# Four image layers on one core: another order of the seven block products and their banks, more background slots in layer 2, first k and v by seven products, order of the last divisions

## Chip, cores and metric

The kernel runs on one core of one Trainium2 chip. The metric is the device time of one execution in microseconds, the median of three runs. TensorE's granted clock was 0.995 of full speed in the profiled run.

## What is computed

The input x has 4 images of 512 channels and 1024 positions, all in four byte floats. Four layers change it in turn, and each adds its result to x:

- Layer 0: attention with 8 heads of 64 channels, with biases; then an output projection.
- Layer 1: linear attention with 64 softplus features. `KV = Kf V^T`, `wval = Qf KV / (Qf sum(Kf))`, V scaled by a gate of maximum plus mean of x; x becomes `x + gamma * wval`.
- Layer 2: layer norm over channels, attention with one head of 512, projection.
- Layer 3: group norm (32 groups), attention with 4 heads of 128, projection.

```python
qkv = xs @ Wp.T + bp                       # layers 0, 2, 3: three 512x512 products an image
attn = softmax(q @ k.T * hd ** -0.5)
x = x + (attn @ v) @ Wo.T + bo
```

A projection of one image is a product of a 512x512 weight with a 512x1024 activation.

## The kernel before, in words

**Tiles.** x of all four images stays on the chip. A *block* is 128 x 4 x 512: one weight, or half an image (512 positions) of q, k, v or of a normalised x; there are 12 block buffers. Exponentials lie in five `pt` tiles of 128 x 2 x 512. In PSUM there are two `acc` tiles of one bank, two `sc` tiles of two banks each, two `tr` tiles of one bank. A wait for an sc tile is for the whole tile of two banks.

**Projections by seven products.** `two_by_sevens` (L312) cuts the weight and the activation into 2 x 2 blocks and computes the four result blocks from seven block products, not eight (a form of Strassen's method). The list `SEVEN` (L264) says for each product: its number, its bank, whether the result is put (copied, by ScalarE) or added (by VectorE), and to which block. A bank is not cleared between some products, so that sums build up in it. Each call works on two column blocks (`which` 0 and 1), each with one acc tile as bank 0 and the two halves of an sc tile as banks 1 and 2. Each product is two matmuls for each `which`. `channels_first` (L333) makes q and k and, with its own put and add, the output projection `project_out` (L403); `tokens_first` (L352) makes v, with 256 columns a matmul. The sums of weight blocks come from `weight_sums` (L271; four VectorE operations), in layers 0 and 3 once a weight and kept in DRAM (`keep_sums`, L373); the sums of activation blocks come from `right` (L295; four VectorE operations of 128 x 1024, lines 303 to 306).

**The first image of layer 0** uses `first_qkv` (L217), with plain products: q and k of the first half are built in all eight banks at once, chunk by chunk as x, wq and wk arrive; then v of that half, then q, k and v of the second half, four matmuls a bank.

**Attention** (L442). A step is 128 keys of a head pair (layer 0), or 256 keys of a head. In `run`, two steps of scores are issued (L470), then the values (L503) of the two steps before; ScalarE makes the exponential (L477), VectorE adds the exponentials up (L481, L485). When a head is done, `normalize` (L549) is put off by two slots: `denominators` (L529) sums over partitions with a matmul, takes the reciprocal (L541), checks the denominators into `stat` (L542) and returns; then the values are multiplied (L552), which frees their acc tile. With one head (layer 2), `values_of_one` (L512) makes the four output blocks from four steps at once (L518) and divides them (L525). On the last half of the last image the output projection is plain: three of four chunks for each output block, `flush()` of what was put off, then the fourth chunk.

**Background work.** Layer norm, group norm, linear attention and the preparation of layer 3's weights are generators; `slot()` (L155) runs the first in the list by one step. Slots lie between products, between attention steps and in `values_of_one`. `finish()` runs what is left. A layer norm needs 13 steps for an image, a group norm 8, `prepare` (L897) 17. A scheduler then orders the instructions of each engine by their dependences and by its own estimate of times[...].

Of the kernel before, what the change touches and what calls it, by code (L numbers as in the profile page):

```python
# [17 lines left out]
P = 128  # L18
B = 4
C = 512  # L20
# [34 lines left out]
def conv_fast(ctx: ExitStack, tc: tile.TileContext, d: dict, out: bass.AP, flag):  # L55
# [47 lines left out]
    cols = const.tile([P, NCOLS], F32, name="cols")  # L103
    nc.sync.dma_start(cols, d["cols"])
    w0 = [block(n) for n in ("wq", "wk", "wv")]
    for c in range(NC):
        nc.sync.dma_start(xs[0][:, c, :TB], xin[0, :, c, :TB])
        for w, part in ((w0[0], 0), (w0[1], 1)):
            nc.sync.dma_start(w[:, c, :], by_chunk(d["wqkv0"])[:, c, part * C : (part + 1) * C])
    nc.sync.dma_start(w0[2], by_chunk(d["wqkv0"])[:, :, 2 * C : 3 * C])  # L110
    nc.sync.dma_start(xs[0][:, :, TB:], xin[0, :, :, TB:])
    wo = load("wo", d["wo0"])
    for b in range(1, B):
        nc.sync.dma_start(xs[b], xin[b])
# [99 lines left out]
        else:  # L214
            nc.vector.tensor_copy(dst, ps)

    def first_qkv(w, bias, xb):  # L217

        q, k, v = [], [], []
        for tb in range(NTB):
            x = xb[tb]
            q.append(block("q"))
            k.append(block("k"))
            v.append(block("v"))
            if tb == 0:

                banks = [s[:, i, :] for s in (sc_tile(), sc_tile()) for i in range(2)]
                banks += [acc_tile() for _ in range(2)] + [tr_tile() for _ in range(2)]
                for c in range(NC):
                    for o in range(2 * NC):
                        product(
                            banks[o], lambda c: w[o // NC][:, c, bass.ts(o % NC, P)],
                            lambda c: x[:, c, :], [c],
                        )
                for o in range(2 * NC):
                    evict(o, (q, k)[o // NC][tb][:, o % NC, :], banks[o], col(bias, o))  # L240
            else:
                for o in range(2 * NC):
                    ps = acc_tile()
                    product(
                        ps, lambda c: w[o // NC][:, c, bass.ts(o % NC, P)], lambda c: x[:, c, :]
                    )
                    slot()
                    evict(o, (q, k)[o // NC][tb][:, o % NC, :], ps, col(bias, o))
            for t in range(QT):
                ps = acc_tile()  # L250
                product(ps, lambda c: x[:, c, bass.ts(t, P)], lambda c: w[2][:, c, :])
                slot()
                evict(t, v[tb][:, t, :], ps)
        return q, k, v

# [4 lines left out]


    SEVEN = [  # L264
        (1, 0, "put", (0, 0)), (2, 1, "add", (0, 0)), (7, 2, "put", (1, 1)), (6, 0, "put", (1, 0)),
        (4, 2, "add", (1, 0)), (5, 0, "add", (1, 1)), (3, 0, "put", (0, 1)),
    ]
    HC = NC // 2
    HO = C // 2
# [42 lines left out]
    def two_by_sevens(factors, n, put, add):  # L312


        banks = []
        for _ in range(2):
            pair_of = sc_tile()
            banks.append([acc_tile()[:, :n], pair_of[:, 0, :n], pair_of[:, 1, :n]])
        for i, bank, do, block_of in SEVEN:
            for which in range(2):  # L320
                ps = banks[which][bank]
                for j in range(HC):
                    lhs, rhs = factors(which, i, j)

                    first = i in (1, 2, 7)
                    nc.tensor.matmul(  # L326
                        ps, lhsT=lhs, rhs=rhs, start=first and j == 0, stop=(j == HC - 1),
                        skip_group_check=not first,
                    )
                (put if do == "put" else add)(which, block_of, ps)  # L330
            slot()

    def channels_first(a, b, out, put=None, bias=None):  # L333
# [39 lines left out]
    def keep_sums(key, w):  # L373

        t = weight_sums(w, "wsum")
        kept = dram.tile([P, NC, TB], F32, tag=key, name="kept")
        nc.sync.dma_start(kept, t)
        sums_in_dram[key] = kept

    def load_left(key, src, part=0):  # L380
        w = load("w", src, part)
# [21 lines left out]
    def project_out(att, a):  # L403


        b = right(att.q, [lambda: pair("t3"), lambda: pair("t2"), pt_tile], over=True)

        def put(which, at, ps):
            o = 2 * at[0] + which
            att.add_to_x(at[1], o, ps, done=(at == (0, 1)))  # L410

        def add(which, at, ps):
            o = 2 * at[0] + which
            xv = xs[att.b][:, o, bass.ts(at[1], TB)]
            nc.vector.tensor_tensor(xv, ps, xv, ALU.add)
            att.store_x(at[1], o)

        def factors(which, i, j):
            return a[i][:, j, bass.ts(which, P)], b[i][:, j, :]

        two_by_sevens(factors, TB, put, add)

    def project_qkv(loads, bias, xb, before):

        x = right(xb, [pt_tile] * 4)
        q = [block("q") for _ in range(NTB)]
        channels_first(loads.take("q"), x, q, bias=lambda o: col(bias, o))
        if before is not None:
            loads.start("k")
            project_out(before, loads.take("o"))  # L430
            loads.start("v")
        else:
            loads.start("v")
        if before is not None and before.then is not None:
            background.append(before.then())
        k = [block("k") for _ in range(NTB)]
        channels_first(loads.take("k"), x, k, bias=lambda o: col(bias, NC + o))
        v = [block("v") for _ in range(NTB)]
        tokens_first(loads.take("v"), x, v)
        return q, k, v  # L440

    class Attention:  # L442
# [69 lines left out]
        def values_of_one(s, i):  # L512
            qb, g, j = s.steps[i]
            parts = [s.pts.pop(i - s.per + 1 + n) for n in range(s.per)]
            for n in range(NC):
                ps = acc_tile()
                for key in range(NT):
                    nc.tensor.matmul(  # L518
                        ps, lhsT=s.v[key // QT][:, key % QT, bass.ts(n, P)],
                        rhs=parts[key // 2][:, key % 2, :],  # L520
                        start=(key == 0), stop=(key == NT - 1),
                    )
                if n == 0:
                    r = s.denominators(qb, g)
                nc.vector.tensor_tensor(ps, ps, r, ALU.mult)  # L525
                s.add_to_x(qb, n, ps)
                slot()

        def denominators(s, qb, g):  # L529
            t = s.sums.pop((qb, g))  # L530
            ps = tr_tile("den")
            if s.pair:
                for half in range(2):
                    nc.tensor.matmul(  # L534
                        ps[half * s.hd : (half + 1) * s.hd, :], lhsT=ones[:, : s.hd],
                        rhs=t[:, half, :], start=True, stop=True,
                    )
            else:
                nc.tensor.matmul(ps, lhsT=ones, rhs=t[:, 0, :], start=True, stop=True)  # L539
            r = work.tile([P, TB], F32, tag="r", bufs=2, name="r")  # L540
            nc.vector.reciprocal(r, ps)  # L541
            nc.vector.scalar_tensor_tensor(  # L542
                ps, ps, 0.0, r, ALU.add, ALU.add,
                accum_out=stat[:, n_units[0] : n_units[0] + 1],
            )
            n_units[0] += 1
            return r

        def normalize(s, qb, g):  # L549

            r = s.denominators(qb, g)
            nc.vector.tensor_tensor(s.q[qb][:, g, :], s.accs.pop((qb, g)), r, ALU.mult)  # L552
            if s.last and g == s.groups - 1 and qb < NTB - 1:
                later(3, lambda: s.project_out(qb))

# [21 lines left out]
        def run(s):  # L577


            for i in range(0, len(s.steps) + 2, 2):  # L580
                for n in range(i, i + 2):
                    if n < len(s.steps):
                        s.scores(n)
                for n in range(i - 2, i):
                    if n >= 0:
                        s.values(n)
                if not s.one or i % s.per:
                    slot()
            if s.last:

# [1 line left out]
                banks = [t[:, i, :] for t in (sc_tile(), sc_tile()) for i in range(2)]  # L592
                for o in range(NC):
                    s.out_product(banks[o], s_last, o, range(NC - 1))
                flush()
                for o in range(NC):
                    s.out_product(banks[o], s_last, o, [NC - 1])
                    s.add_to_x(s_last, o, banks[o])
# [234 lines left out]
        norms[key] = []  # L833
        background.append(norm(b, norms[key]))

    def idle(n):
        for _ in range(n):
            yield


# [2 lines left out]
    for b in range(B):  # L843
        xb = [xs[b][:, :, bass.ts(tb, TB)] for tb in range(NTB)]
        if b == 0:
            for key, w in zip(("q0", "k0", "v0", "o0"), w0 + [wo]):
                keep_sums(key, w)
            q, k, v = first_qkv(w0, "bqkv0", xb)
            eb = column_sums(wo, "bqkv0", 2, "bo0")
            wv1 = load("wv1", d["wv1"])  # L850
            w1 = block("w1")
# [60 lines left out]
    for b in range(B):  # L912
# [7 lines left out]
            finish()  # L920
            start_norm(layer_norm, b + 1, f"ln{b + 1}")
        else:
            start_norm(group_norm, 0, "gn0")
            background.append(prepare())
        Attention(b, q, xn, v, 1, None, eb).run()
        finish()

# [501 lines left out]
```

## Time and profile before

The median is 2649.06 us (2648.99 to 2651.49); the profiled execution took 2642.78 us, its span on the core 2641.1 us.

| part of the profile | busy or total |
|---|---|
| VectorE, ScalarE | 1410.6 us (53%), 690.1 us (26%) |
| chain that ended last: TensorE, VectorE, ScalarE, issue | 92%, 4%, 2%, 1% |
| block products of all projections in the chain (L326) | 18% + 12% |
| reciprocals of denominators (L541), 72 of 3356 ns | 241.7 us |
| data moved | 100.44 MB, 38 GB/s in the mean |

PE is TensorE, DVE is VectorE, ACT is ScalarE, SP issues most transfers. In a row such as `acc<-ptt,ws` the tile before the arrow is written. A row of the table of waits reads: engine, tile and line that waited `<-` engine, tile and line that ended the wait. A row of the timeline gives start, length, engine, line, operation, tiles and shapes, and in brackets the idle time before it. A matmul leaves two records.

### The profile page before, as it was taken

The numbers are of one execution on the slowest core, as the hardware profiler recorded it, in microseconds if no ns is written. First come the engines' busy times: TensorE is split into PE (matmuls) and PEld (weight loads), VectorE is DVE, ScalarE is ACT, GpSimd is POOL, SyncE is SP. The second block draws the span as 40 slices with busy tenths as digits, with TensorE's granted clock in tenths as the row PEclk, the third lists the DMA queues.
The fourth block names the chain that finished last, engine by engine and source line by source line (L and its number), as shares of the span: only waits on it lengthen the run. The fifth ranks groups of instructions, "written<-read, shape, count | busy, mean of one in ns | idle before, by whom it ended". The sixth has DMA issues, their size and how long they took to land.

```text
span 2641.1 us, 19557 instructions
## 1 busy us (share of the span) xinstructions
PE 2584.7 (98%) x7818; PEld 1174.1 (44%) x7818; DVE 1410.6 (53%) x1637; ACT 690.1 (26%) x881; POOL 2.1 (0%) x12
## 2 busy tenths in 40 slices
PE   9999999999999999999999999989999999999998
PEld 4333533353335334544544545435445444544543
DVE  2486477646864887426345153252762563365254
ACT  0342244134412541212211112012321321231220
POOL 0000000000000000000000000000000000000000
PEclk9999999999999999999999999999999999999999
DMA  8001000100010001000000000041012002102000
GB/s 310 33 1 64 32 32 1 64 32 32 1 64 32 0 1 64 1 0 0 1 0 0 1 0 32 16 175 64 0 48 80 32 32 80 48 0 96 16 0 33
DMA packets 35953, 100.44 MB, mean 38 GB/s; under 512 B 2448, under 2 KB 2960, under 8 KB 31248
## 3 DMA queue, kind: packets, MB, share of 16 engines
q1 hardware_dynamic: 33552, 94.94, 10.0%
q10 hardware_dynamic: 2304, 4.20, 0.4%
q8 instruction: 63, 1.03, 0.2%
q14 instruction: 34, 0.28, 0.0%
HBM read 82.35 MB, written 16.78 MB: 38 GB/s over the span
## 4 chain that ended last, share of the span: by engine, by line
PE 92%; DVE 4%; ACT 2%; issue 1%; DMA 0%; SPq 0%; DVEq 0%; ACTq 0%
PE sc L470 25%; PE acc L326 18%; PE acc L503 17%; PE sc L326 12%; PE acc L518 8%; PE acc L202 3%; PE den L539 1%; PE sc L202 1%; PE z L628 1%; PE den L534 1%; PE wval L730 1%; PE kx L675 1%; DVE sum L485 1%; PE xtr L666 1%; PE po L202 1%
## 5 line engine op out<-in xcount | busy, mean ns | idle before, releaser
L477 ACT ACTIVATE ptt<-sc 128x1024 f32<-128x1024 f32 x416 | 411.9, 1022 | 748.3 <-PE sc L470 697.9
L470 PE MATMUL sc<-q,k 64*128 64x512 f32 (+1 forms) x1536 | 486.6, 610 | 7.2 <-ACT ptt L477 7.1
L503 PE MATMUL acc<-ptt,v 128*64 128x512 f32 (+1 forms) x1536 | 478.8, 603 | 0.0
L485 DVE TENSOR_TENSOR sum<-sum,ptt 128x1024 f32<-128x1024 f32 x272 | 331.1, 1217 | 231.3 <-ACT ptt L477 221.2
L470 PEld LDWEIGHTS sc<-q,k 64*128 64x128 f32 (+1 forms) x1536 | 184.5, 187 | 288.8 <-issue 197.9
L541 DVE RECIPROCAL r<-den 128x512 f32<-128x512 f32 x72 | 241.7, 3356 | 125.8 <-PE den L539 123.3
L503 PEld LDWEIGHTS acc<-ptt,v 128*64 128x64 f32 (+1 forms) x1536 | 160.0, 154 | 293.3 <-issue 290.7
L518 PE MATMUL acc<-ptt,v 128*128 128x512 f32 x512 | 223.7, 592 | 0.3 <-DVE x L567 0.3
L470 PE MATMUL sc<-q,ln 128*128 128x512 f32 x512 | 221.1, 592 | 0.0
L481 DVE TENSOR_TENSOR sum<-ptt 128x1024 f32<-128x1024 f32 x72 | 87.8, 1219 | 154.4 <-ACT ptt L477 154.2
L518 PEld LDWEIGHTS acc<-ptt,v 128*128 128x128 f32 x512 | 97.1, 190 | 122.6 <-issue 120.8
L470 PEld LDWEIGHTS sc<-q,ln 128*128 128x128 f32 x512 | 97.2, 190 | 120.3 <-issue 120.1
L367 DVE TENSOR_TENSOR v<-sc,v 128x256 f32<-128x256 f32 x88 | 37.3, 424 | 144.8 <-PE sc L326 143.1
L326 PE MATMUL acc<-ptt,ws 128*128 128x512 f32 x224 | 102.5, 595 | 0.0
L363 ACT COPY v<-acc 128x256 f32<-128x256 f32 x132 | 48.7, 372 | 148.1 <-PE acc L326 148.1
L344 ACT ACTIVATE k<-acc,cols 128x512 f32<-128x512 f32 x42 | 28.9, 687 | 215.2 <-PE acc L326 215.2
L567 DVE SCALAR_TENSOR_TENSOR x<-acc,cs,x 128x512 f32<-128x512 f32 x74 | 55.4, 749 | 51.9 <-PE acc L326 51.3
L326 PE MATMUL sc<-ptt,w 128*128 128x512 f32 x168 | 76.6, 594 | 0.0
L344 ACT ACTIVATE q<-acc,cols 128x512 f32<-128x512 f32 x42 | 28.9, 687 | 175.7 <-PE acc L326 175.7
L326 PEld LDWEIGHTS acc<-ptt,ws 128*128 128x128 f32 x224 | 42.1, 190 | 55.2 <-issue 50.7
L348 DVE TENSOR_TENSOR q<-sc,q 128x512 f32<-128x512 f32 x44 | 29.9, 679 | 68.1 <-PE sc L326 68.1
L348 DVE TENSOR_TENSOR k<-sc,k 128x512 f32<-128x512 f32 x28 | 19.4, 691 | 81.4 <-PE sc L326 81.4
(265 smaller groups left out, 2557.7 us busy)
## 6 DMA issues: line engine op xcount, KB each, us to landing
ws<-kept SPq DMA_DIRECT2D x28, 1024.0 KB, 4.8
w<-in_wqkv SPq DMA_DIRECT2D x24, 1024.0 KB, 5.0
kept<-wsum SPq DMA_DIRECT2D x8, 1024.0 KB, 10.1
w<-in_wo SPq DMA_DIRECT2D x7, 1024.0 KB, 5.3
x<-in_x SPq DMA_DIRECT2D x3, 2048.0 KB, 20.4
wo<-in_wo SPq DMA_DIRECT2D x4, 1024.0 KB, 6.3
out<-x SPq DMA_DIRECT2D x16, 256.0 KB, 2.0
out<-x ACTq DMA_DIRECT2D x16, 256.0 KB, 2.0
```

The source lines that it names most:

```text
L202: nc.tensor.matmul(ps, lhsT=lhs(c), rhs=rhs(c), start=(c == 0), stop=(c == NC - 1))
L326: nc.tensor.matmul(ps, lhsT=lhs, rhs=rhs, start=first and j == 0, stop=(j == HC - 1), skip_group_check=not first,)
L344: nc.scalar.activation(out[at[1]][:, o, :], ps, AF.Identity, bias=bias(o))
L348: nc.vector.tensor_tensor(c, ps, c, ALU.add)
L470: nc.tensor.matmul(ps[:, half, :], lhsT=s.k[key // QT][p0:p1, c, bass.ts(key % QT, P)], rhs=s.q[qb][p0:p1, c, :], start=(n == 0), stop=(n ...
L477: nc.scalar.activation(pt, ps, AF.Exp, scale=s.scale)
L481: nc.vector.tensor_tensor(t, s.pts[i - 1], pt, ALU.add)
L485: nc.vector.tensor_tensor(t, t, pt, ALU.add)
L503: nc.tensor.matmul(ps[p0:p1, :], lhsT=s.v[key // QT][:, key % QT, g * P + p0 : g * P + p1], rhs=pt[:, half, :], start=(key == 0), stop=(ke ...
L518: nc.tensor.matmul(ps, lhsT=s.v[key // QT][:, key % QT, bass.ts(n, P)], rhs=parts[key // 2][:, key % 2, :], start=(key == 0), stop=(key == ...
L541: nc.vector.reciprocal(r, ps)
L567: nc.vector.scalar_tensor_tensor(xv, ps, s.eb[:, o : o + 1], xv, ALU.add, ALU.add)
```

## The change

1. **Order and banks of the seven products.** The list begins with product 2. Product 3 gets a cleared bank 1 (it was added up in bank 0), product 5 comes last and its sum in bank 0 is added to two result blocks. So a call has four additions for each `which`, not three, and four copies as before. The aim is to have other products between the eviction of a tile and its next use. In `project_out` the store of the second half now follows the addition.
2. **First k and v by seven products.** `first_qkv` becomes `first_q`: q of both halves is built in the eight banks, chunk by chunk, and k and v come from `channels_first` and `tokens_first`. x of the first image is loaded in whole chunks.
3. **More slots in layer 2.** A slot after each score step and none after the values: 16 an image instead of 10. After the last image group norm and weight preparation advance side by side (`together`), one step of each in a slot.
4. **Last divisions.** The multiplication stands before the check everywhere (`check` is a function of its own), and at the very end the flush stands behind the first output block's three chunks.

```diff
-    SEVEN = [
-        (1, 0, "put", (0, 0)), (2, 1, "add", (0, 0)), (7, 2, "put", (1, 1)), (6, 0, "put", (1, 0)),
-        (4, 2, "add", (1, 0)), (5, 0, "add", (1, 1)), (3, 0, "put", (0, 1)),
-    ]
+    SEVEN = [
+        (2, 1, [("put", (0, 0))]), (1, 0, [("add", (0, 0))]), (7, 2, [("put", (1, 1))]),
+        (6, 0, [("put", (1, 0))]), (4, 2, [("add", (1, 0))]), (3, 1, [("put", (0, 1))]),
+        (5, 0, [("add", (1, 1)), ("add", (0, 1))]),
+    ]
...
-                    first = i in (1, 2, 7)
+                    more = i in (4, 5, 6)
...
-            att.add_to_x(at[1], o, ps, done=(at == (0, 1)))
+            att.add_to_x(at[1], o, ps, done=False)
...
     for c in range(NC):
-        nc.sync.dma_start(xs[0][:, c, :TB], xin[0, :, c, :TB])
-        for w, part in ((w0[0], 0), (w0[1], 1)):
-            nc.sync.dma_start(w[:, c, :], by_chunk(d["wqkv0"])[:, c, part * C : (part + 1) * C])
...
+        nc.sync.dma_start(xs[0][:, c, :], xin[0, :, c, :])
+        nc.sync.dma_start(w0[0][:, c, :], w0v[:, c, :C])
...
+    def first_q(w, bias, xb):
+        q = [block("q") for _ in range(NTB)]
+        banks = [s[:, i, :] for s in (sc_tile(), sc_tile()) for i in range(2)]
+        banks += [acc_tile() for _ in range(2)] + [tr_tile() for _ in range(2)]
+        for c in range(NC):
+            for n in range(2 * NC):
+                product(
+                    banks[n], lambda c: w[:, c, bass.ts(n // NTB, P)],
+                    lambda c: xb[n % NTB][:, c, :], [c],
+                )
...
-            q, k, v = first_qkv(w0, "bqkv0", xb)
+            q = first_q(w0[0], "bqkv0", xb)
+            x = right(xb, [pt_tile] * 4)
+            k = [block("k") for _ in range(NTB)]
+            channels_first(
+                left(w0[1], keep_sums("k0", w0[1])), x, k, bias=lambda o: col("bqkv0", NC + o)
+            )
+            v = [block("v") for _ in range(NTB)]
+            tokens_first(left(w0[2], keep_sums("v0", w0[2])), x, v)
+            keep_sums("q0", w0[0])
+            keep_sums("o0", wo)
...
                 if n == 0:
-                    r = s.denominators(qb, g)
+                    den, r = s.denominators(qb, g)
                 nc.vector.tensor_tensor(ps, ps, r, ALU.mult)
                 s.add_to_x(qb, n, ps)
+                if n == 0:
+                    s.check(den, r)
...
-            r = s.denominators(qb, g)
+            den, r = s.denominators(qb, g)
             nc.vector.tensor_tensor(s.q[qb][:, g, :], s.accs.pop((qb, g)), r, ALU.mult)
+            s.check(den, r)
...
                         s.scores(n)
+                        if s.one:
+                            slot()
...
-                if not s.one or i % s.per:
+                if not s.one:
                     slot()
...
                 for o in range(NC):
                     s.out_product(banks[o], s_last, o, range(NC - 1))
-                flush()
+                    flush()
...
-            start_norm(group_norm, 0, "gn0")
-            background.append(prepare())
+            norms["gn0"] = []
+            background.append(together(group_norm(0, norms["gn0"]), prepare()))
```

More of the change, by code (lines that the diff above doesn't have):

```diff
@@ L105, in conv_fast @@
     w0 = [block(n) for n in ("wq", "wk", "wv")]
+    w0v = by_chunk(d["wqkv0"])
     for c in range(NC):
-        nc.sync.dma_start(xs[0][:, c, :TB], xin[0, :, c, :TB])
-        for w, part in ((w0[0], 0), (w0[1], 1)):
-            nc.sync.dma_start(w[:, c, :], by_chunk(d["wqkv0"])[:, c, part * C : (part + 1) * C])
-    nc.sync.dma_start(w0[2], by_chunk(d["wqkv0"])[:, :, 2 * C : 3 * C])
-    nc.sync.dma_start(xs[0][:, :, TB:], xin[0, :, :, TB:])
+        nc.sync.dma_start(xs[0][:, c, :], xin[0, :, c, :])
+        nc.sync.dma_start(w0[0][:, c, :], w0v[:, c, :C])
+    for part in (1, 2):
+        nc.sync.dma_start(w0[part], w0v[:, :, part * C : (part + 1) * C])
     wo = load("wo", d["wo0"])
@@ L215, in evict @@
             nc.vector.tensor_copy(dst, ps)
[L217 to L254, printed above, removed]
@@ new lines, in first_q @@
+    def first_q(w, bias, xb):
[8 more added lines that the diff above has]
+                )
+        for n in range(2 * NC):
+            evict(n, q[n % NTB][:, n // NTB, :], banks[n], col(bias, n // NTB))
+        return q
@@ L318, in two_by_sevens @@
             banks.append([acc_tile()[:, :n], pair_of[:, 0, :n], pair_of[:, 1, :n]])
-        for i, bank, do, block_of in SEVEN:
+        for i, bank, uses in SEVEN:
             for which in range(2):
@@ L323, in two_by_sevens @@
                     lhs, rhs = factors(which, i, j)
-                    first = i in (1, 2, 7)
+                    more = i in (4, 5, 6)
                     nc.tensor.matmul(
-                        ps, lhsT=lhs, rhs=rhs, start=first and j == 0, stop=(j == HC - 1),
-                        skip_group_check=not first,
-                    )
-                (put if do == "put" else add)(which, block_of, ps)
+                        ps, lhsT=lhs, rhs=rhs, start=not more and j == 0, stop=(j == HC - 1),
+                        skip_group_check=more,
+                    )
+                for do, block_of in uses:
+                    (put if do == "put" else add)(which, block_of, ps)
             slot()
@@ L378, in keep_sums @@
         sums_in_dram[key] = kept
+        return t
     def load_left(key, src, part=0):
@@ L541, in denominators, with check @@
             nc.vector.reciprocal(r, ps)
+            return ps, r
+        def check(s, den, r):
             nc.vector.scalar_tensor_tensor(
-                ps, ps, 0.0, r, ALU.add, ALU.add,
+                den, den, 0.0, r, ALU.add, ALU.add,
                 accum_out=stat[:, n_units[0] : n_units[0] + 1],
@@ L546, in denominators @@
             n_units[0] += 1
-            return r
         def normalize(s, qb, g):
-            r = s.denominators(qb, g)
+            den, r = s.denominators(qb, g)
             nc.vector.tensor_tensor(s.q[qb][:, g, :], s.accs.pop((qb, g)), r, ALU.mult)
+            s.check(den, r)
             if s.last and g == s.groups - 1 and qb < NTB - 1:
@@ L834, in start_norm, with together @@
         background.append(norm(b, norms[key]))
-    def idle(n):
-        for _ in range(n):
+    def together(*parts):
+        parts = list(parts)
+        while parts:
+            parts = [p for p in parts if next(p, "end") != "end"]
             yield
@@ L845, in conv_fast @@
         if b == 0:
-            for key, w in zip(("q0", "k0", "v0", "o0"), w0 + [wo]):
-                keep_sums(key, w)
-            q, k, v = first_qkv(w0, "bqkv0", xb)
+            q = first_q(w0[0], "bqkv0", xb)
[8 more added lines that the diff above has]
+            keep_sums("o0", wo)
             eb = column_sums(wo, "bqkv0", 2, "bo0")
```

## Prediction

> **What bounds the kernel now.** I read the page first, then TensorE's own table of waits, then the chain of waits and the timeline around each wait.
>
> ```profile
> PE 2584.7 (98%) x7818; PEld 1174.1 (44%) x7818; DVE 1410.6 (53%) x1637; ACT 690.1 (26%) x881; POOL 2.1 (0%) x12
> ```
>
> TensorE is busy for 98% of the span and VectorE for 53%: time goes only with matmuls or with TensorE's idle gaps. The gaps, in the table of waits of TensorE alone:
>
> ```profile
> PE sc L326 <- DVE ptt L303: 11.2, 3, 3.8
> PE acc L326 <- DMA w<-in_wqkv: 7.5, 1, 7.5
> PE sc L470 <- ACT ptt L477: 7.1, 7, 2.9
> PE sc L202 <- DMA wq<-in_wqkv: 5.3, 1, 5.3
> PE sc L202 <- DVE q L552: 4.8, 1, 4.8
> PE sc L326 <- DVE q L348: 4.2, 3, 1.4
> PE acc L326 <- ACT v L363: 3.4, 4, 0.9
> PE sc L326 <- DVE v L367: 2.6, 3, 0.9
> PE nd L720 <- DVE z L611: 1.5, 1, 1.5
> ...
> PE acc L326 <- DVE v L367: 0.7, 1, 0.7
> PE csum L190 <- DVE cs L187: 0.4, 1, 0.4
> ```
>
> Columns are the total in us, the count, the longest. They sum to some 50 us: the most that better order alone can give. For the matmul part, the chain of waits and the timeline of layer 3 (start, us, what):
>
> ```profile
> 34.47 54.93 PE acc L202 x128
> ...
> 2027.19 3.60 PE L326 MATMUL acc<-gn,ws 128*128 128x512 f32 x8
> 2030.63 2.07 PE L326 MATMUL acc<-w,gn 128*128 128x256 f32 x8
> 2032.54 1.89 PE L326 MATMUL sc<-w,gn 128*128 128x256 f32 x8
> 2034.26 1.89 PE L326 MATMUL sc<-ws,ptt 128*128 128x256 f32 x8
> ```
>
> Each matmul leaves two records [...], so x128 is 64 matmuls in 54.93 us: 0.858 us for 512 columns. By start to start, the four matmuls of one block product take 3.43 us at 512 columns and 1.73 us at 256.
>
> [...] the 4.2 us of line 348 come where the product that follows uses the tile just evicted. [...] here w takes 5.0 us from issue to landing, and the stretch 6 to 16 us runs at 362 GB/s.
>
> **The change part by part.**
>
> *First k and v by seven products.* Removed: the 64 matmuls of 54.93 us (v twice, q and k of the second half). q alone now fills the opening phase, again with 32 matmuls. Added: k, 7 x 3.43 = 24.0 us, and v, 14 x 1.73 = 24.2 us. Net -6.7 us. The opening needs 512 KB of x and 256 KB of wq before its first matmul instead of 256 + 256: 256 KB at 362 GB/s is +0.7 us. The sums come from VectorE: four of x (1.2 us each, row L303's 128x1024) and four per weight (0.6 us apart). VectorE was idle until 13.47 us; x is complete after 3 MB, about 14 us, so the x sums end near 19 us, the column sums of wo, which follow, near 27 us, and q is evicted from about 30 us (29.36 before, plus the 0.7). The wk sums stand between these evictions, 2.4 us in all, before the third product of k. I take no wait here. Saving the q and o sums for the next batch has until about 200 us: free.
>
> *More slots in layer 2.* An image had 2 + 8 = 10 slots for a layer norm that needs 13 steps; the last three ran in `finish()`, with TensorE waiting for line 303. Timeline of VectorE there:
>
> ```profile
> 1255.92 3.35 DVE L779 RECIPROCAL rstd<-rstd 128x512 f32<-128x512 f32 x1
> ...
> 1259.73 2.73 DVE L782 SCALAR_TENSOR_TENSOR ln<-ln,cols,rstd 128x512 f32<-128x512 f32 x4
> 1262.37 0.69 DVE L348 TENSOR_TENSOR q<-sc,q 128x512 f32<-128x512 f32 x1
> 1262.97 1.22 DVE L303 TENSOR_TENSOR ptt<-ln 128x1024 f32<-128x1024 f32 x1
> ```
>
> Now there are 8 + 8 = 16 slots. In the changed order the second half's sum of squares stands before the last two score steps: 2 x 6.87 + 6.87 + 0.86 + 3 x 6.87 = 42 us of TensorE work ahead of the next projection, against 3.4 + 2.7 + 1.2 us of VectorE. The three waits of 3.8 go: -11.2. Does the work pulled forward delay the division there? The first half's rstd chain (3.35 + 2.7 us) starts after score step 4, and the denominators come 21 us later, behind two more score steps and eight value matmuls: no. Division, check and add behind them take 3.35 + 0.7 + 0.84 + 0.75 = 5.6 us, against the 6.87 us of matmuls until that bank is wanted. Table switches do not increase: eight loads for the square root in both programs.
>
> *Group norm beside weight preparation.* After the last image they ran one after the other, 25 steps, so TensorE waited 7.5 us for the first weights of layer 3 and 0.4 for the column sums. Side by side they fit: the weight load now stands behind the third part's sums, about 50 us before the projection, and takes 5 us. -7.9.
>
> *Last divisions.* At the end TensorE waits 4.8 us for reciprocal, check and multiplication. With the flush behind the first output block, nine matmuls (7.7 us) lie under 3.36 + 0.7 us: -4.8. Multiplying before the check hastens every division by 0.84 us, but elsewhere nobody waits for it.
>
> *Order of the seven.* Before, three reuses of a tile followed directly on its eviction: 7 behind the addition of 2 (same two-bank sc tile), 3 behind that of 5, the next call's 1 behind the copy of 3. Then only the other half's matmuls (1.72 us, at 256 columns 0.86) cover the eviction. After, one is left: 3 behind the addition of 4. Price: two more additions per call, 0.69 or 0.42 us, 58 and 60 calls of the instruction in all including the first k and v, some 65 us more on an engine idle for 47%; they are hidden by the next call's product 2, which uses another bank. Where waits stand:
> - Start of q in layer 0 (three times 1.4). TensorE now runs 2, denominators, half of 1, all of 7, then the other half of 1, whose bank the last division frees. With the start at 217.5 us: 7 ends at 227.0; reciprocal from 222.4 to 225.7, one addition, multiplication until 227.0. No wait; but the addition of the second half of 1 stands behind two sums of q and the half of 6 that needs it waits about 0.3 us. 4.2 becomes 0.9: -3.3.
> - v beside linear attention (ACT v 3.4, DVE v 2.6 and 0.7, nd 1.5: 8.2 us in four places). Product 1 no longer waits for the copies that stand behind two table loads, nor 7 for the additions behind softplus. But then `nd` comes up earlier than its z, and waits some 0.8 us; the last place keeps about 1.8. 8.2 becomes 4.2: -4.0.
> - First exponentials after v in batches 1 to 3 (0.88 each, among the 7.1): the table load stood behind the copies of product 3, which are now one product earlier. Perhaps 0.3 is left: -1.8.
>
> **Sum.** -6.7 + 0.7 - 11.2 - 7.9 - 4.8 - 3.3 - 4.0 - 1.8 = -39.0 us; 2649.1 - 39.0 = 2610.1, rounded to 2610. Each wait also costs about 0.15 us of restart (start-to-start excess over the listed gap), some 2 us more for fourteen; I set them against small new waits, as at 3 behind 4 in the busy stretches.
>
> **Rivals.**
> - VectorE starts to bind where work was pulled forward (chance 0.16): a reciprocal of 3.35 us or a layer norm's additions catch an eviction now and then. For it: 65 us more VectorE work, and slices of the page where VectorE is at 8 tenths. Against it: layer 3 ran with the same adjacent reuses without a gap. About 0.4 us in each of 26 calls: +10, so 2620.
> - The order removes nearly all waits (0.10): only the opening and a handful of ACT waits (5 us) are left of the 50, with restarts: 2649 - 6.0 - 40 - 1 = 2602.
> - Slower (0.03): the one adjacent reuse, 3 behind the addition of 4, is uncovered in every call, with VectorE in the middle of a reciprocal: about 2 us in 26 calls of 512 columns = 52 us against the 39: 2662. Against it: VectorE idles 0.96 us between evictions throughout layer 3's projections.
> - My reading: 0.71, 2610.
>
> **Numbers.** The range takes in the first three: low 2601, high 2624 (the rival of 2620 and, on the unknown side, no gain at all from the seven's order, +9, and 5 us of new waits). Chances: faster 0.96, same 0.01, slower 0.03.
>
> **What would show it.** Right: TensorE's waits for line 303 under 1 us in all; no DMA wait but the opening one; no wait for the last q; the waits of the projections at some 5 us; the span some 39 us shorter; TensorE's matmul time 6.7 us less. Wrong: waits of TensorE for VectorE additions spread over all projections; a wait for line 525's or 552's multiplication in layer 2; DMA waits in layer 3 or at the first k.

## The result, and the profile after

The changed kernel takes 2589.53 us in the median (2588.38 to 2590.26) against 2650.12 us for the kernel before (2648.99 to 2651.49): a ratio of 0.9771 (95% interval 0.9754 to 0.9788), 60.6 us faster. The forecast was 2610.0 us, 39.0 us faster than the 2649.06 it started from, with a range of 2601 to 2624. The direction was right, and the gain was half as large again as forecast.

From the page of the changed kernel, busy time of each engine (share of the span, instructions):

```profile
PE 2563.6 (99%) x7858; PEld 1182.5 (46%) x7858; DVE 1465.4 (57%) x1751; ACT 696.7 (27%) x897; POOL 2.1 (0%) x12
```

VectorE has 55 us more work than before (1410.6 us), near the 65 us forecast, and does not bind. The waits of TensorE alone, after (total us, times, longest):

```profile
PE sc L202 <- DMA wq<-in_wqkv: 5.8, 1, 5.8
PE nd L712 <- DVE z L603: 3.9, 3, 1.3
PE sc L455 <- ACT ptt L462: 3.9, 5, 2.9
PE sc L304 <- DVE v L346: 2.1, 1, 2.1
PE wval L722 <- DVE x L727: 0.6, 3, 0.2
PE csum L190 <- DVE cs L187: 0.4, 1, 0.4
```

They sum to 16.7 us, where the same table of before sums to 49.8: 33.1 us of waiting are gone. The prediction took away 33.0 us of waits (11.2 + 7.9 + 4.8 + 3.3 + 4.0 + 1.8), before the 0.7 us that it added for the opening. What was promised by name is there: nothing for the sums of the layer norm (line 303, now 281), no transfer but the opening one, no wait for the last q. The timeline of TensorE at the first boundary of layer 2 runs without a gap:

```profile
1224.81 10.89 PE L503 MATMUL acc<-ptt,v 128*128 128x512 f32 x25
1235.54 3.60 PE L304 MATMUL sc<-ln,wqk 128*128 128x512 f32 x8
1238.97 3.60 PE L304 MATMUL acc<-ln,wqk 128*128 128x512 f32 x8
1242.40 3.60 PE L304 MATMUL sc<-ptt,wqks 128*128 128x512 f32 x8
```

and so does the end:

```profile
2565.32 2.74 PE L202 MATMUL sc<-q,wo 128*128 128x512 f32 x6
2567.89 1.02 PE L526 MATMUL den<-sum,ones 128*128 128x512 f32 x2
2568.75 9.61 PE L202 MATMUL sc<-q,wo 128*128 128x512 f32 x22
```

So the waits account for their forecast share, and the 21.6 us between 39.0 and 60.6 came from somewhere that the table of waits does not show. The matmuls behind the gaps of the kernel before show where. Timeline of TensorE, kernel before, at two of the three waits of 3.8 us; both rows are the same eight matmul records of product 7:

```profile
1264.25 5.40 PE L326 MATMUL sc<-ptt,wqks 128*128 128x512 f32 x8 [3.83 <-DVE ptt L303]
...
1433.44 3.70 PE L326 MATMUL sc<-ptt,wqks 128*128 128x512 f32 x8 [3.83 <-DVE ptt L303]
```

Behind the same gap, the first group took 5.40 us and the second 3.70. The view of stretches (busy time and instructions of each engine, then TensorE's granted clock, the DMA share and GB/s) gives the difference:

```profile
core 0: us, PE busy (x) PEld busy (x) DVE busy (x) ACT busy (x) POOL busy (x), PEclk, DMA share, GB/s
...
1264.00:1270.00 6.00, 5.75 (x10) 2.50 (x11) 4.32 (x6) 1.01 (x2) 0.00 (x0) 0.72 0.01 3
...
1433.00:1440.00 7.00, 6.55 (x16) 2.97 (x17) 4.49 (x5) 2.06 (x3) 0.00 (x0) 1.00 0.00 0
```

The clock granted to TensorE was down behind one gap (0.72 over 6 us) and full behind the other (1.00 over 7 us). A busy share cannot show this: TensorE was busy for 5.75 of those 6 us, while the records of the first group at half clock start 853 ns apart, against 429 ns in the second group.

### The profile page after: what moved, and what is told of

Read it like the earlier page. It is cut to its first block, busy times and chain, and to the rows that moved or that the text cites. A ratio compares the mean times of both kernels' runs of the same rounds, so it can differ in the third digit from the quotient of the medians.

```text
span 2587.5 us, 19776 instructions
## 1 busy us (share of the span) xinstructions
PE 2563.6 (99%) x7858; PEld 1182.5 (46%) x7858; DVE 1465.4 (57%) x1751; ACT 696.7 (27%) x897; POOL 2.1 (0%) x12
## 3 DMA queue, kind: packets, MB, share of 16 engines
q1 hardware_dynamic: 32976, 94.94, 10.3%
## 4 chain that ended last, share of the span: by engine, by line
PE 96%; DVE 2%; ACT 1%; issue 1%; DMA 0%; SPq 0%; DVEq 0%
PE sc L455 26%; PE sc L304 20%; PE acc L488 17%; PE acc L304 15%; PE acc L503 8%; PE den L526 1%; PE sc L202 1%; PE z L620 1%; PE acc L202 1%; PE den L521 1%; PE wval L722 1%; PE kx L667 1%; PE xtr L658 1%; PE po L202 1%; PE kv L202 1%
## 5 line engine op out<-in xcount | busy, mean ns | idle before, releaser
L342 ACT COPY v<-sc 128x256 f32<-128x256 f32 x144 | 53.3, 372 | 218.4 <-PE sc L304 217.9
L323 ACT ACTIVATE k<-sc,cols 128x512 f32<-128x512 f32 x48 | 33.0, 688 | 260.4 <-PE sc L304 260.4
L346 DVE TENSOR_TENSOR v<-acc,v 128x256 f32<-128x256 f32 x144 | 56.2, 420 | 71.3 <-PE acc L304 63.4
L327 DVE TENSOR_TENSOR q<-acc,q 128x512 f32<-128x512 f32 x66 | 43.1, 682 | 72.1 <-PE acc L304 72.1
L327 DVE TENSOR_TENSOR k<-acc,k 128x512 f32<-128x512 f32 x48 | 31.6, 687 | 65.8 <-PE acc L304 60.9
L323 ACT ACTIVATE q<-sc,cols 128x512 f32<-128x512 f32 x42 | 28.9, 687 | 148.1 <-PE sc L304 148.1
L346 DVE TENSOR_TENSOR v<-sc,v 128x256 f32<-128x256 f32 x48 | 20.3, 424 | 71.8 <-PE sc L304 71.7
## 6 DMA issues: line engine op xcount, KB each, us to landing
x<-in_x SPq DMA_DIRECT2D x3, 2048.0 KB, 19.1
```

The costliest lines, as they stand in the source:

```text
L323: nc.scalar.activation(out[at[1]][:, o, :], ps, AF.Identity, bias=bias(o))
L327: nc.vector.tensor_tensor(c, ps, c, ALU.add)
L346: nc.vector.tensor_tensor(c, ps, c, ALU.add)
```

## The experiments

Three theories stood, and the expectations below name them by letter. **A** is the prediction's own bookkeeping: a wait costs its idle time, and the restart is small. **B**: the clock falls in the longer gaps and the matmuls behind them pay. **C**: the old order of the seven products lost time at every reuse of a tile, below what the table of waits lists. Each part of the change was first made alone, on the kernel before. The difference given is that of the medians; the range in brackets comes from the 95% interval of the ratio.

### The order of the seven alone

```diff
-        for i, bank, do, block_of in SEVEN:
+        for i, bank, uses in SEVEN:
...
-            att.add_to_x(at[1], o, ps, done=(at == (0, 1)))
+            att.add_to_x(at[1], o, ps, done=False)
```

with the new list `SEVEN` and nothing else of the change.

> The kernel before with only the new order of the seven products and their banks (both projections of all layers that used it; first k and v as before). Theory A, the terms on record: 3.3 (start of q in layer 0) + 4.0 (v beside linear attention) + 1.8 (first exponentials) = 9.1 us faster, 2641. Theory B, TensorE restarts slowly after each of its gaps, the clock falling after the long ones: here only short gaps go, so 9 to 12 us faster. Theory C, the old order had small stalls at every reuse of a tile, which the list of waits doesn't show: some 20 us faster, spread over all 26 calls with 512 columns and the others.

Measured: 2634.05 against 2650.24 us, ratio 0.9941 (0.9927 to 0.9954), 16.2 us faster (12.2 to 19.3). More than A, less than C. Its profile shows the listed waits as forecast: the start of q in layer 0 waits no more, ScalarE's copies and the exponentials lost 5.0 us of waits, and `nd` gained:

```profile
PE sc L472 <- ACT ptt L479: 5.5, 7, 2.9
...
PE nd L722 <- DVE z L613: 3.9, 3, 1.3
PE sc L327 <- DVE v L369: 2.1, 1, 2.1
```

The rest is small and spread out. I summed, over the matmuls that use all 128 rows and columns, how much later than normal the next matmul started (normal is 429 ns after a record of 512 columns, 216 after one of 256, 109 after one of 128). Delays under one half-clock step and without a listed wait sum to 17.3 us in the profile of before and 14.0 in this one; delays beyond the listed gap, at the gaps themselves, to 4.9 us at 27 gaps (0.18 each) and 3.1 at 16. So theory C is right in kind, at some 3.3 us and not 10, and each gap removed brings some 0.18 us with it. With the 7.4 us by which the listed waits fell, this makes 12.5 us, and the two profiled spans, both at a mean clock of 0.995, differ by 12.0. The rest of the 16.2 goes with the clock: in this comparison no execution of the kernel before was above 0.993, and two of the five with the new order ran at 0.995.

### The slots of layer 2 alone

```diff
                         s.scores(n)
+                        if s.one:
+                            slot()
...
-                if not s.one or i % s.per:
+                if not s.one:
                     slot()
...
+            norms["gn0"] = []
+            background.append(together(group_norm(0, norms["gn0"]), prepare()))
```

> The kernel before with only the new slots of layer 2 and group norm beside the weight preparation. Theory A: the three waits of 3.8 us and the waits of 7.5 and 0.4 us go, 19.1 us faster, 2631. Theory B: with each wait of over 3 us a stretch of slower clock goes too, some 1.8 us for each of the three in layer 2 if it happens each time, 2 to 4 us behind the DMA wait: 25 to 29 us faster, 2621 to 2625. Theory C: 19 us faster, as A.

Measured: 2617.6 us, ratio 0.9881 (0.9866 to 0.9896), 32.6 us faster (27.6 to 35.5). A and C fall. B's expectation was 25 to 29, too low mainly because its price of one stretch behind a 3.8 us wait, 1.8 us, came from the one stretch that the profile of before happened to have; the next run shows about 3.

### First q, k and v alone

```diff
-            q, k, v = first_qkv(w0, "bqkv0", xb)
+            q = first_q(w0[0], "bqkv0", xb)
+            x = right(xb, [pt_tile] * 4)
...
+            tokens_first(left(w0[2], keep_sums("v0", w0[2])), x, v)
```

> The kernel before with only the first q in the opening phase and first k and v by seven products, in the old order of the seven. Theory A: 64 matmuls of 0.858 us become 28 of it and 56 of 0.43 us, -6.7, +0.7 for the larger opening: 6.0 us faster, 2644. Theory B: the same[...]; up to 1 us less if the reuse in the old order catches the copies of the new calls. Theory C: about 4 us faster, since two calls with the stalls of the old order are added.

Measured: 2644.68 us, ratio 0.9981 (0.9972 to 0.9989), 5.6 us faster (2.9 to 7.4). As forecast by A. This kernel still has the gaps of before, and its profile shows the full price. The same group of matmuls in the timeline:

```profile
1428.26 6.67 PE L303 MATMUL sc<-ptt,wqks 128*128 128x512 f32 x8 [3.83 <-DVE ptt L280]
```

and the stretches behind all five gaps (three of layer 2, before layer 3, the last q):

```profile
1258.00:1264.00 6.00, 6.00 (x8) 2.64 (x9) 4.06 (x5) 0.69 (x1) 0.00 (x0) 0.53 0.00 0
1428.00:1434.00 6.00, 5.74 (x7) 2.53 (x8) 4.30 (x5) 0.69 (x1) 0.00 (x0) 0.50 0.00 0
1599.00:1605.00 6.00, 6.00 (x8) 2.39 (x9) 3.30 (x3) 0.69 (x1) 0.00 (x0) 0.50 0.00 0
1764.00:1772.00 8.00, 7.64 (x15) 3.73 (x15) 2.15 (x4) 0.69 (x1) 0.00 (x0) 0.50 0.92 327
2631.00:2637.00 6.00, 5.88 (x10) 2.50 (x10) 2.41 (x6) 0.00 (x0) 0.00 (x0) 0.60 0.18 72
```

Half clock behind every one. The matmuls there start late by 2.9, 3.1, 3.2, 2.8 and 2.5 us in all. With these prices the slots alone should bring 19.1 (waits) + 9.2 (behind the three of layer 2) + 2.8 (before layer 3) + 0.9 (five restarts of 0.18) = 32.0 us, and 32.6 was measured (27.6 to 35.5).

### The last divisions alone

```diff
             nc.vector.tensor_tensor(s.q[qb][:, g, :], s.accs.pop((qb, g)), r, ALU.mult)
+            s.check(den, r)
...
-                flush()
+                    flush()
```

> The kernel before with only the multiplication ahead of the check and the last flush behind the first output block. Theory A: the wait of 4.8 us for the last q goes, 4.8 us faster, 2645. Theory B: the slower clock behind it (1.9 us in the profile of before) goes as well: 6.7 us faster, 2643. Theory C: 4.8 us.

Measured: 2640.64 us, ratio 0.9966 (0.9954 to 0.9978), 9.6 us faster (5.8 to 12.2). A falls; B's 6.7 us is inside. The wait of 4.8 us and the 2.5 us behind it make 7.3; the small unlisted delays are some 1 to 2 us less as well, by the sum used above (records that fall into a change of the clock make it uncertain).

### Filling the gaps without ending a wait

If theory B holds, filling the gaps should gain time although no wait ends earlier. Dummy matmuls, whose results nobody reads, were put into the gaps of the kernel before (the first image of layer 2 has no such gap and gets none):

```diff
+    def fill(n, rhs):
+        ps = tr_tile("fill")
+        for _ in range(n):
+            nc.tensor.matmul(ps, lhsT=ones, rhs=rhs, start=True, stop=True)
...
+            if i == 2 and fills:
+                fill(fills, xs[0][:, 0, :TB])
...
+        if b == B - 1:
+            fill(7, xs[0][:, 0, :TB])
         finish()
...
                 flush()
+                fill(5, xs[0][:, 0, :TB])
```

> The kernel before with dummy matmuls (a tile of x times ones, result unused) placed where TensorE would idle: four before product 7 of the first projection of images 1 to 3 in layer 2 (3.43 us of the 3.8), seven before layer 3 (one of them lands earlier, in the last attention), five behind the last flush. No wait ends earlier and no useful work goes. Theory A (a wait costs its idle time only): the same time, or up to 1 us slower through the one that lands early. Theory B (the clock falls in these gaps and costs some 3 us in each of the five): 10 to 14 us faster, 2636 to 2640, and no stretch with a clock under 0.9 behind them.

Measured: 2641.2 against 2649.26 us, ratio 0.9972 (0.9961 to 0.9983), 8.1 us faster (4.5 to 10.3), by adding 24 useless matmuls. A falls: the dummies do no useful work. The boundary of layer 2 in its timeline:

```profile
1260.99 3.60 PE L315 MATMUL fill<-x,ones 128*128 128x512 f32 x8
1264.98 3.70 PE L331 MATMUL sc<-ptt,wqks 128*128 128x512 f32 x8 [0.40 <-DVE ptt L303]
```

Product 7 begins no earlier than before (1264.25), but runs at full rate. B's 10 to 14 us were missed because the stretch before layer 3 stayed (2.65 us): waits of 1.7 us for the weights and 1.3 us for the column sums remained around two matmul records. So the seven dummies there were made nine:

```diff
-            fill(7, xs[0][:, 0, :TB])
+            fill(9, xs[0][:, 0, :TB])
```

> The kernel with dummy matmuls of the earlier experiment, with nine instead of seven ahead of layer 3, so that the wait of 1.7 us that was left for the weights shrinks to about 0.1 and only the 1.3 us for the column sums stay. If the slow stretch there came of two short waits close together (1.7 and 1.3 us within 5 us), it goes: some 2.6 us less than with seven, 2638.5. If it comes of something else (the one-column matmuls of the column sums, the transfer running beside), it stays: 2641, as with seven.

Measured: 2637.88 against 2649.02 us, ratio 0.9957 (0.9944 to 0.9971). The median is 3.3 us below that with seven, but the intervals overlap, and in the profile the stretch is shorter, not gone:

```profile
1758.00:1762.00 4.00, 3.45 (x8) 1.06 (x6) 3.93 (x8) 0.00 (x0) 0.00 (x0) 1.00 0.57 222
1762.00:1768.00 6.00, 5.22 (x15) 2.67 (x16) 0.89 (x2) 0.69 (x1) 0.00 (x0) 0.72 1.00 348
```

So two close waits are not needed there: the clock also fell behind one wait of 1.3 us, with eight one-column records after it and a transfer beside it (DMA share 1.00). Which of these it takes was not separated.

### How long a gap must be

The changed kernel with 30 gaps of chosen length at its end (one execution), each followed by 18 dummy matmuls of 512 columns:

```diff
+    def gap(us):
+        prev = tr_tile("gap")
+        nc.tensor.matmul(prev, lhsT=ones, rhs=xs[0][:, 0, :TB], start=True, stop=True)
+        t = row("gap")
+        nc.vector.tensor_copy(t, prev)
+        for _ in range(us):
+            nc.vector.tensor_scalar(t, t, 1.0, None, ALU.mult)
+        ps = tr_tile("gap")
+        nc.tensor.matmul(ps, lhsT=ones, rhs=t, start=True, stop=True)
+        fill(18, xs[0][:, 0, :TB])
```

> The changed kernel with 30 added stretches at its end, each a gap of TensorE of a chosen length (a chain of VectorE operations, 0 to 14 of them, whose end TensorE waits for) and then 18 dummy matmuls of 512 columns; three times through ten lengths. Theory A: each gap costs its length plus 0.15 to 0.2 us at any length. Theory B: from a length between 1.4 and 2.9 us on (the waits of 1.4 us show no slow stretch, that of 2.9 us does) the matmuls behind the gap run at half speed for some microseconds, 2 to 3 us lost each, not always for the shorter ones.

From its timeline, the first pass; the bracket has the gap, the second number the length of the two records behind it (1.10 at full rate, 2.04 at half):

```profile
2658.44 1.10 PE L956 MATMUL gap<-gap,ones 128*128 128x512 f32 x2 [2.72 <-DVE gap L954]
...
2679.03 1.10 PE L956 MATMUL gap<-gap,ones 128*128 128x512 f32 x2 [3.18 <-DVE gap L954]
...
2700.08 1.10 PE L956 MATMUL gap<-gap,ones 128*128 128x512 f32 x2 [3.65 <-DVE gap L954]
...
2722.06 2.04 PE L956 MATMUL gap<-gap,ones 128*128 128x512 f32 x2 [4.57 <-DVE gap L954]
2723.89 16.37 PE L946 MATMUL fill<-x,ones 128*128 128x512 f32 x36
```

All three passes, from start to start of the records (29 gaps: the first did not open, since matmuls of the last projection were put into it):

| gap, us | passes with records at half rate | lost behind the gap, us |
|---|---|---|
| 0.8 to 2.7 | 0 of 14 | 0.1 |
| 3.18 | 1 of 3 | 2.9 |
| 3.65 | 2 of 3 | 2.9, 1.8 |
| 4.6 to 7.3 | 9 of 9 | 1.7 to 3.1 |

A slow record takes 853 ns from start to start in place of 429, some three to seven in a row. The loss is there or not, and from 4.6 to 7.3 us of gap it did not grow.

What looks like chance between 3.2 and 3.8 us may be the place of the gap in time. In the profile of the kernel before, the granted clock was at half for 6.83, 3.41, 10.24 and 3.41 us, from 905.94, 1264.34, 1759.27 and 2629.67 us: one, two or three times 3.41 us. The four starts lie whole multiples of that apart as well (105, 145 and 255 times 3.4133 us). Here the kernel before is cut at these multiples, at the first two of its waits of 3.8 us (columns as in the view of stretches above):

```profile
1260.93:1264.34 3.41, 0.09 (x1) 0.10 (x1) 3.41 (x6) 0.00 (x0) 0.00 (x0) 1.00 0.00 0
1264.34:1267.75 3.41, 3.41 (x4) 1.36 (x5) 3.41 (x5) 0.00 (x0) 0.00 (x0) 0.50 0.00 0
1267.75:1271.16 3.41, 3.41 (x9) 1.52 (x8) 0.57 (x1) 1.37 (x2) 0.00 (x0) 1.00 0.02 5
...
1428.18:1431.60 3.42, 1.44 (x4) 0.37 (x2) 3.42 (x7) 0.00 (x0) 0.00 (x0) 1.00 0.00 0
1431.60:1435.01 3.41, 1.56 (x4) 0.85 (x5) 3.41 (x5) 0.00 (x0) 0.00 (x0) 1.00 0.00 0
1435.01:1438.42 3.41, 3.41 (x9) 1.50 (x9) 2.48 (x3) 1.38 (x2) 0.00 (x0) 1.00 0.00 0
```

The first gap lies almost whole in one row (TensorE busy for 0.09 of 3.41 us), and the next row runs at half clock. The second, as long, is cut in half (busy for 1.44 and 1.56 us), and the clock stays full. That the place decides for gaps of this length is an estimate of mine from these two gaps; how much idle time it takes was not shown.

The sweep stands for dense work alone. The wait of 2.9 us in attention, among matmuls of 64 rows or 64 columns, was followed by half clock in each of nine profiles (the granted clock was 0.50 to 0.85 in the two stretches of 4 us behind it), while of the three gaps of 3.18 us in the sweep one was.

### The gaps that the changed kernel still has

Two repairs on the changed kernel: dummies in the opening, where TensorE waits 5.8 us for its first data, and one more step before the layer norm's squares, which on ScalarE stood ahead of an exponential (the wait of 2.9 us): in the changed kernel ScalarE idles for 6.19 us until VectorE delivers to the norm, squares from 886.16 us, and begins the exponential at 887.30.

```diff
+        fill(14, ones)
         q = [block("q") for _ in range(NTB)]
```

> The changed kernel with 14 dummy matmuls of 128 columns in the opening, while TensorE waits for the first transfers. Theory A: no change, 2589.5. Theory B: the first matmuls start at full clock, 2.4 us faster, 2587.

Measured: 2586.59 us, ratio 0.9769 (0.9755 to 0.9783) to the kernel before, against 0.9771 for the changed kernel: the intervals overlap, the medians differ by 2.9 us. The timelines show 2.3 of it (the group ends at 11.83 and at 9.49 us). First group of the changed kernel:

```profile
5.82 6.01 PE L202 MATMUL sc<-x,wq 128*128 128x512 f32 x8 [5.82 <-DMA wq<-in_wqkv]
```

and with the dummies:

```profile
1.11 4.93 PE L220 MATMUL fill<-ones 128*128 128x128 f32 x28 [1.11 <-DVE ones L124]
5.89 3.60 PE L202 MATMUL sc<-x,wq 128*128 128x512 f32 x8
```

The second repair:

```diff
+            if b == 0:
+                yield
             var = total(square)
```

> The changed kernel with one more step before the squares of the first layer norm, so that ScalarE's exponentials of the last attention of layer 1 do not queue behind squares that wait for VectorE. Theory A: the wait of 2.9 us goes, 2586.7. Theory B: the stretch of half clock behind it goes as well (the matmuls of 888 to 896 us take some 3 us more than their like): 6 us faster, 2583.5.

Measured: 2588.6 us, ratio 0.9776 (0.9762 to 0.9789). Not the 6 us: no gain that these runs can tell. At the place itself it worked, as the stretches behind the wait show; the denominators there come 6.1 us earlier. Changed kernel, then the repaired one:

```profile
890.00:896.00 6.00, 6.00 (x18) 1.56 (x16) 3.96 (x4) 3.59 (x4) 0.00 (x0) 0.62 0.00 0
```

```profile
890.00:896.00 6.00, 4.07 (x18) 1.09 (x16) 5.97 (x9) 5.50 (x8) 0.00 (x0) 1.00 0.00 0
```

But 3.6 us came back within the next 40 us. The waits that replaced the one removed are shorter, but more:

```profile
PE sc L455 <- ACT ptt L462: 3.0, 6, 1.1
...
PE den L521 <- DVE sum L470: 0.9, 1, 0.9
```

A further 1.7 us came back at 1093 us: behind a wait of 2.08 us that both kernels have, seven records of 256 columns took 427 ns each in this execution and 216 in that of the changed kernel (granted clock 0.92 and 1.00 from 1080 to 1100 us). This part is chance and not the repair: with both repairs, below, the added step is there as well, and eight such records behind that wait take 1.89 us, the full rate.

Both repairs together:

> The changed kernel with the 14 dummy matmuls of the opening and the additional step before the first layer norm's squares together. If the two add up: 2.9 us and 0.9 us below the changed kernel, 2585.7. If the slow stretch that followed the 2.1 us wait at 1095 us in the run with the additional step alone was chance, up to 1.5 us less, 2584. Theory A (no clock) has no gain from the dummy matmuls and 0.9 from the step: 2588.6.

Measured: 2585.08 us (2584.7 to 2585.89), ratio 0.9757 (0.9743 to 0.977), the fastest kernel here; all its runs lie below all runs of the changed one (2588.38 to 2590.26). This is 4.4 us below the changed kernel, where 3.8 was expected if the parts add; the matmuls behind the 2.08 us wait ran at full rate this time.

## Why the prediction was right and wrong

**Right: first k and v.** -6.7 + 0.7 was forecast; alone it gave 5.6 us.

**Right: which waits go, and how far.** Line 303, the weights of layer 3, the last q: as worked out, from the slots, the 42 us of matmuls ahead of the norm's end, and the nine matmuls over the last division. In the sum for the order of the seven, single terms missed in both directions: the 0.9 us left at the start of q in layer 0 is zero, `nd` waits 1.3 us three times and not 0.8, the last place 2.1 and not 1.8, and the exponentials lost 3.2 us of waits and not 1.8. Together the listed waits fell by 33.1 us for 33.0; that the sum is right to 0.1 us is in part luck.

**Right: VectorE does not bind**, and the rival of 2620 us and the slower one fall: the five other waits of the table sum to 10.9 us, with none spread over the projections. The rival in which nearly all waits go, to 5 us, falls too: 16.7 us are left. It gave 2602 us, still too long, for it had the same price of a gap.

**Wrong: the price of a wait.** The step that failed is the sentence on restarts: "Each wait also costs about 0.15 us of restart (start-to-start excess over the listed gap), some 2 us more for fourteen; I set them against small new waits." So the sum counted a wait as its idle time and put what stands behind it at nothing; half clock does not occur in it. The 0.15 us fits short waits (0.18 us at a gap in before); where half clock followed one of the five long ones, 1.7 to 3.2 us were measured, and delays without a listed wait were left out altogether. The sums over full-array matmuls in the two profiled executions:

| us | before | after |
|---|---|---|
| delays at the listed gaps, beyond them | 4.9 | 1.3 |
| small delays with no listed gap | 17.3 | 11.5 |
| records at half rate | 6.8 | 2.4 |

That is 3.6 + 5.8 + 4.4 = 13.8 us, which with 33.1 (waits) and 6.7 (fewer matmuls) gives 53.6, the difference of the two spans (2641.1 and 2587.5). The measured 60.6 us are 6.9 more, and these go with the clock too, as the next paragraph shows. So of the 21.6 us that the forecast missed, some 11 (4.4 + 6.9) are the clock; the cause of the 5.8 us of small delays stays open.

**The rest: the profiled execution of before was a lucky one.** It took 2642.8 us with a mean clock of 0.995. In 47 later executions of the same kernel the times go with the clock: three at 0.995 took 2642.9 to 2643.2 us, twenty at 0.993 took 2648.7 in the median, twenty-one at 0.991 took 2650.5 (the other three, at 0.992, took 2651.1). In the profile only one of the three waits of layer 2 was followed by half clock; in that of first q, whose mean clock was 0.991, all three were, and at 2.9 to 3.2 us each, two more would make up the step from 2643 to 2649. The profile of before has 23.9 us at half clock up to 2639.91 us; by the means, 0.993 and 0.991 stand for about 37 and 48 us (an estimate: twice the missing share of 2649 us). Behind which gaps they lay, the executions without a profile cannot show. The changed kernel has none of these gaps, and ran at 0.998 to 0.999 each time. I had both numbers, 2649.06 for the median and 2642.78 for the profile, and did not ask what the 6 us were.

The four parts alone sum to 64.0 us, the whole to 60.6: within their intervals they add.

## What to carry to other kernels

A gap of the tensor engine in dense work cost its length here, and 1.7 to 3.2 us more where half clock followed: in the sweep behind none of 14 gaps up to 2.7 us, behind three of six of 3.18 and 3.65, and behind all nine from 4.6 to 7.3. Read the granted clock behind each gap, and price a removed gap with both. Ending the gap is worth most, but where the data cannot come earlier, dummy matmuls in the gap save the second part (8 us here over five gaps). When median and profile differ, compare their mean clocks before taking durations from the profile: the one profile of before has half clock behind one of three equal gaps, that of first q behind all three.

## What the runs showed of the hardware

- Dummy matmuls that nobody reads made the kernel before 8.1 us faster (4.5 to 10.3).
- In the profile of the kernel before the granted clock was at half for 6.83, 3.41, 10.24 and 3.41 us, at or behind waits of 2.9, 3.8, 7.5 and 4.8 us; behind the two other waits of 3.8 us it stayed full.
- The loss behind a gap of the sweep was a step: 0.1 us up to 2.7 us of gap, 1.7 to 3.1 us from 4.6 to 7.3. In one pass of 3.65 us it began late: the first two records took 1.10 us, as at full rate, and the 36 behind them 17.31 us in place of 15.61.
- Matmuls often started some 0.1 us late with no listed wait: 189 times in the kernel before, 17.3 us in all. Another order of the seven products alone took away 43 of them and 3.3 us. What causes each of the others is open.
- Fewer waits in a table are not a shorter time: one more step took away a wait of 2.9 us and 3 us of half clock, and smaller waits and a new slow stretch gave nearly all of it back in the profiled execution.
